# A macaron block with relative-position attention on one core: earlier value loads, last stores on two queues, means kept unnegated

## The chip, the cores and the metric

The kernel runs on one core of a Trainium2 chip. A core has a matrix engine (PE, with its weight loads listed as PEld), a vector engine (DVE), an activation engine (ACT), a general engine (POOL) and SP, which in this kernel only issues DMA transfers. Each engine works through its own list of instructions in order; semaphores make one engine wait for another or for a transfer. The metric is the time of one execution in microseconds of the device; the figure for a kernel is the median over runs. The profile is one execution, recorded by the hardware profiler.

## The reference

The input x has the shape (8, 1024, 256): 8 sequences of 1024 rows, 256 columns, in 32-bit floats. One block is computed, of three parts with a residual each:

```
x = x + 0.5 * ffn(layernorm(x))
x = x + attn(layernorm(x))
x = x + 0.5 * ffn(layernorm(x))

layernorm(x): (x - mean) / sqrt(var + 1e-5), over the 256 columns
ffn(y):  tanh(y @ W1 @ W2 @ W3 + bias)
attn(y): y = layernorm(y) * g + b;  q, k, v = y @ Wq + bq, y @ Wk + bk, y @ Wv + bv   (16 heads of 16)
         p = sinusoidal_positions @ Wp
         score = ((q + u_bias) . k  +  shift((q + v_bias) . p)) / 4
         softmax(score) @ v, heads put together, @ Wo + bo
```

`shift` is the reshaping trick in which a column of zeros is put before the position scores, the array is read with rows one longer, and the first row is dropped. The scores of one head are 8 x 1024 x 1024 numbers.

## The kernel before

**First stage (to about 300 us).** Eight groups of 128 rows of all 8 sequences are loaded (`load_x`, L250). A `Stats` object (L257) holds the layer norm's statistics of a group: DVE computes mean and variance (`bn_stats`, `bn_aggr`), and in `ends` (L269) a DVE instruction (L272) writes the negated means into a tile `n`; POOL computes 1/sqrt(var + eps) in two instructions (`rsqrt`, L104 to L106). `apply` (L284) lets POOL write (x + n) * r, one instruction for each of the 8 sequences, with n and r as per-partition scalars. This is done twice for each group ("a" ahead of the first feed-forward part, "b" ahead of the attention), 16 times in all. POOL also clears the tiles of the attention stage here (`UnitSet.clear`, L138, memsets at L140 and L143), and adds a constant row vector to x (L384). Queries, keys and values go to DRAM (qv_d, k_d, v_d), the residual goes to x1c_d.

**Attention stage.** A unit is one head with one quarter (row group `rg`) of the query rows: 64 units of 16 steps, so 1024 steps T. `step` (L1023) computes the scores of step T+2 in PSUM on PE, takes their row maxima on DVE (L934, L940, L947), and lets ACT exponentiate (L963) the scores of step T into the tile eT. `step` also issues one item of the list `loads` in each row maximum (`row_max`, L943): SP's transfers of the next unit's data, each made to follow that step's DVE reduction (L950). `fetch` (L1012) fills the list at the first step of each unit: six keys' transfers in five items, two items of position data, two of the values (`v`, 256 KB each, into the tile vt) and four of queries. In the last unit there is no next unit, so `k`, `p` and `q` are empty; the slices of them still are appended, as three empty items, and the values come as the fourth and fifth item. At the first step of the following unit, `emit_av` (L983) multiplies eT by vt on PE (L971), ACT copies the sums (L978) and SP stores them in h_d (L992). The values' tile has one buffer, so a unit's values are loaded after the unit before has been multiplied. While later units run, `post_ops` (L754) finishes the blocks (one of 8 sequences of one row group each, 32 in all) of the row group before: normalise by the softmax sums, output projection, residual, layer norm (`stats_dve`, L108, with the negated means at L117, and `apply`, L812), second feed-forward part, store.

**Last unit and last blocks (from L1072).** After step 1009 (the second of the last unit) SP gets, in program order, the load of the softmax sums of 15 heads (rc, L1075), the numerators of heads 0 to 7 (tn, L1087); then step 1010 runs; DVE inverts rc (L1094), SP stores it in r_d (L1095), loads the other numerators (tn), both sets of inverted sums (td, L1100, which wait for r_d) and the residual rows of the 8 last blocks (xr, L1106, in `load_rows` L728, 16 transfers of 128 KB). Then come steps 1011 to 1023. After them the last unit's av is formed in two halves of 4 sequences (L1136), and each half's 16 sums and 16 inverses are moved to the other heads' tiles by 4 + 4 small SP transfers (L1141, L1144). POOL multiplies numerators by inverses (L1117, and L1172 for the last heads), ACT and DVE split them into two 16-bit parts (L1123, L1129, L1173), PE projects them (`proj`, L1155). The 8 last blocks then pass through the remaining operations of `post_ops` as a pipeline (L1182 to L1191): DVE adds and takes statistics, POOL normalises, PE transposes and multiplies, ACT takes the tanh, then `fin` (L842) adds the result to xr, on ACT and POOL for blocks 0 to 4 and on DVE for 5 to 7, and `store` (L852) writes out by two SP transfers (`store_rows`, L734), one for each half of its rows, 128 KB each.

The order on each engine is the order in which the Python code calls the instructions; a framework adds the semaphores. DMA transfers use eight semaphores in turn, so that a transfer waits until the one eight places earlier has landed.

Of the kernel before, what the change touches and what calls it, by code (L numbers as in the profile page):

```python
# [10 lines left out]
F32 = mybir.dt.float32  # L11
AF = mybir.ActivationFunctionType
ALU = mybir.AluOpType
# [3 lines left out]
P = 128  # L17
NB = 8
# [14 lines left out]
NU = NTILE // UT  # L33
# [10 lines left out]
def macaron_kernel(  # L44
# [23 lines left out]
    nc = tc.nc  # L68
# [35 lines left out]
    def rsqrt(r, var):  # L104
        nc.gpsimd.tensor_scalar(r, var, 1.0, EPS, ALU.mult, ALU.add)
        nc.gpsimd.tensor_tensor(r, r, mhalf[:, : r.shape[1]], ALU.pow)  # L106

    def stats_dve(pool, xt, n, nm):  # L108
        st = pool.tile([P, n, 6], F32, tag="st" + nm, name="st" + nm)
        mv = pool.tile([P, n, 2], F32, tag="mv" + nm, name="mv" + nm)  # L110
        for b in range(n):
            nc.vector.bn_stats(st[:, b, :], xt[:, b, :])
        for b in range(n):
            nc.vector.bn_aggr(mv[:, b, :], st[:, b, :])
        r = pool.tile([P, n], F32, tag="r" + nm, name="r" + nm)
        nm_ = pool.tile([P, n], F32, tag="n" + nm, name="n" + nm)
        nc.vector.tensor_scalar_mul(nm_, mv[:, :, 0], -1.0)  # L117
        return nm_, r, mv

# [6 lines left out]
    class UnitSet:  # L128
        def __init__(self, pool, n):
            def t(name, shape):  # L130
                return pool.tile(shape, F16, tag=f"{name}{n}", name=f"{name}{n}")

            self.qc = t("qc", [KC, UT, 4, 32])
            self.q = t("q", [KR, UT + 1, NI * NB, 2])
            self.k = t("k", [KC, NI, 4, P])
            self.pg = t("pg", [KR, GW])
# [93 lines left out]
    if True:  # L230
        p2 = early.enter_context(tc.tile_pool(name="p2", bufs=2, side="right"))
# [25 lines left out]
        class Stats:  # L257
            def __init__(self, nm, xt):
                self.nm, self.xt = nm, xt
                self.st = p2.tile([P, NB, 6], F32, tag="st" + nm, name="st" + nm)  # L260
                self.mv = p2.tile([P, NB, 2], F32, tag="mv" + nm, name="mv" + nm)
                self.r = p2.tile([P, NB], F32, tag="r" + nm, name="r" + nm)
                self.n = p2.tile([P, NB], F32, tag="n" + nm, name="n" + nm)

            def rows(self, lo, hi):
                for b in range(lo, hi):
# [2 lines left out]
            def ends(self):  # L269
                for b in range(NB):  # L270
                    nc.vector.bn_aggr(self.mv[:, b, :], self.st[:, b, :])
                nc.vector.tensor_scalar_mul(self.n, self.mv[:, :, 0], -1.0)  # L272
                rsqrt(self.r, self.mv[:, :, 1])

            def again(self):
# [8 lines left out]
            def apply(self, tag):  # L284
                xn = p2.tile([P, NB, D], F32, tag=tag, name=tag, bufs=1)
                for b in range(NB):
                    nc.gpsimd.tensor_scalar(
                        xn[:, b, :], self.xt[:, b, :], self.n[:, b : b + 1],
                        self.r[:, b : b + 1], ALU.add, ALU.mult,
                    )  # L290
                return xn

# [368 lines left out]
        for I in range(NI - 2, -2, -1):  # L661
# [39 lines left out]
            for n in range(4):  # L701
                q = query(xTb, cvst[(I + 1) % 2], n % 2, n // 2)
                k = key(xTb, ks, n % 2, n // 2)
# [27 lines left out]
                t[:, e, :], src.rearrange("(k r) c -> k r c", r=P)[:, r : r + 16]  # L731
            )

    def store_rows(dst, t, rg):  # L734
        for e, r in ((0, 16 * rg), (1, 64 + 16 * rg)):
            nc.sync.dma_start(
                dst.rearrange("(k r) c -> k r c", r=P)[:, r : r + 16], t[:, e, :]
            )

# [14 lines left out]
    def post_ops(rg, b, sb, nb, pm, pt_, t):  # L754
        def new(name, shape, tag=None, dt=F32):
            t[name] = sb.tile(shape, dt, tag=tag or name, name=name, bufs=nb)
            return t[name]

        def load():
            num = new("num", [P, 2, 2 * P])  # L760
            den = new("den", [P, 2, 2 * P])
            for hh in range(2):
                hs = slice(8 * hh, 8 * hh + 8)
                nc.sync.dma_start(num[:, hh, :], h_d[rg, hs, 0:DH, b])
                nc.sync.dma_start(
                    den[:, hh, :],
                    r_d[rg, hs, b : b + 1, :].broadcast_to([8, DH, 2 * P]),
                )
            xr = new("xr", [P, 2, D])
            load_rows(xr, x1c_d[b], rg)  # L770

        def norm():
            nc.gpsimd.tensor_tensor(t["num"], t["num"], t["den"], ALU.mult)

        def hi1():
            new("hl", [P, 2, 2, 2 * P], dt=F16)
            nc.scalar.copy(t["hl"][:, 0], t["num"])

        def lo1():
            nc.vector.tensor_tensor(t["hl"][:, 1], t["num"], t["hl"][:, 0], ALU.subtract)  # L780

        def prod(ps, hl, w, tk, extra):
            n = 0
            for k in range(2):
                for a, c in ((0, 0), (1, 0), (0, 1)):
                    mm(  # L786
                        ps[:, tk, :], hl[:, a, k, tk * P : (tk + 1) * P], w[:, c, k, :],
                        start=n == 0, stop=n == 5 and not extra,
                    )
                    n += 1  # L790

        def proj():
            t["ps"] = pm.tile([P, 2, D], F32, tag=pt_, name="wops")
            for tk in range(2):
                prod(t["ps"], t["hl"], wo16, tk, False)

        def res():
            nc.vector.scalar_tensor_tensor(
                out=t["xr"], in0=t["ps"], scalar=1.0 / WS, in1=t["xr"], op0=ALU.mult,
                op1=ALU.add,  # L800
            )

        def projres():
            proj()
            res()

        def ln():
            if nb > 1:
                res()
            t["nm"], t["r"], t["mv"] = stats_dve(sb, t["xr"], 2, f"p{b % nb}")  # L810

        def apply():  # L812
            rsqrt(t["r"], t["mv"][:, :, 1])
            xn = new("pn", [P, 2, D])
            for k in range(2):
                nc.gpsimd.tensor_scalar(
                    xn[:, k, :], t["xr"][:, k, :], t["nm"][:, k : k + 1],
                    t["r"][:, k : k + 1], ALU.add, ALU.mult,
                )

        def trans():
            t["ps"] = pm.tile([P, 2, 2 * P], F32, tag=pt_, name="ptp")
            for c in range(2):
                for tk in range(2):
                    nc.tensor.transpose(  # L825
                        t["ps"][:, c, tk * P : (tk + 1) * P],
                        t["pn"][:, tk, c * P : (c + 1) * P], ident,
                    )
            new("pT", [P, 2, 2, 2 * P], "hl", F16)
            nc.scalar.copy(t["pT"][:, 0], t["ps"])  # L830
            nc.vector.tensor_tensor(t["pT"][:, 1], t["ps"], t["pT"][:, 0], ALU.subtract)

        def ffn():
            t["ps"] = pm.tile([P, 2, D], F32, tag=pt_, name="pff")
            for tk in range(2):
                prod(t["ps"], t["pT"], w16, tk, True)
                mm(t["ps"][:, tk, :], ones16, brow, start=False, stop=True)
            nc.scalar.activation(
                new("pth", [P, 2, D], "pn"), t["ps"], AF.Tanh, scale=1.0 / WS
            )  # L840

        def fin():  # L842
            if nb > 1 and b < NB - 3:
                nc.scalar.mul(t["pth"], t["pth"], 0.5)
                nc.gpsimd.tensor_tensor(t["xr"], t["xr"], t["pth"], ALU.add)
                return
            nc.vector.scalar_tensor_tensor(
                out=t["xr"], in0=t["pth"], scalar=0.5, in1=t["xr"],
                op0=ALU.mult, op1=ALU.add,
            )  # L850

        def store():  # L852
            store_rows(out[b], t["xr"], rg)

        return [
            (load, 4), (norm, 2), (hi1, 0), (lo1, 1), (projres, 0), (ln, 0), (apply, 4),
            (trans, 1), (ffn, 0), (fin, 1), (store, 1),
        ]

# [147 lines left out]
    preps, loads, stores = [], [], []  # L1007
# [4 lines left out]
    def fetch(u):  # L1012

        v = load_v(u) if u else []
        k, p = (f(u + 1) for f in (sets[(u + 1) % 2].load_k, sets[(u + 1) % 2].load_p)) \
            if u + 1 < NU else ([], [])
        q = sets[u % 2].load_q(u + 2) if u + 2 < NU else []
        loads.extend([pair] for pair in k[0:4])
        loads.append(k[4:6])
        loads.extend((p[0:2], p[2:4], v[0:1], v[1:2]))  # L1020
        loads.extend([pair] for pair in q)
# [51 lines left out]
    rg = units[-1][0]  # L1073
# [4 lines left out]
    def ttile(name, shape, dt=F32, tag=None):  # L1078
        return t1.tile(shape, dt, tag=tag or name, name=name)
# [3 lines left out]
    xr = ttile("xr8", [P, NB, 2, D])  # L1083
# [150 lines left out]
```

## Time and profile before

| | us |
|---|---|
| median of 3 runs | 2954.7 (2951.74 to 2957.57) |
| the profiled execution | 2962.17 |
| its span, first to last instruction | 2960.5 |
| PE busy | 2835.1 (96%) |
| DVE busy | 2188.1 (74%) |
| ACT busy | 1666.0 (56%) |
| POOL busy | 991.9 (34%) |
| mean granted PE clock | 0.984 of full |

Times in the views are from the start of the span. An engine's row names its line in the kernel, the operation, the tile written and the tiles read; "SPq" is SP's list of transfers, and its durations are those of issuing, not of moving the data. The number in brackets is how long the engine was idle before, and what ended that. The table of waits sums such idle times: who waited, for whom, how long, how often. The chain of waits follows the last instruction back to what released each step. A window gives each engine's busy time within a stretch, then the granted clock, the share of time in which the 16 DMA engines were busy, and the GB/s moved.

### The profile page before, as it was taken

The numbers are of one execution on the slowest core, as the hardware profiler recorded it, in microseconds if no ns is written. First come the engines' busy times: TensorE is split into PE (matmuls) and PEld (weight loads), VectorE is DVE, ScalarE is ACT, GpSimd is POOL, SyncE is SP. The second block draws the span as 40 slices with busy tenths as digits, with TensorE's granted clock in tenths as the row PEclk, the third lists the DMA queues.
The fourth block names the chain that finished last, engine by engine and source line by source line (L and its number), as shares of the span: only waits on it lengthen the run. The fifth ranks groups of instructions, "written<-read, shape, count | busy, mean of one in ns | idle before, by whom it ended". The sixth has DMA issues, their size and how long they took to land.

```text
span 2960.5 us, 157394 instructions
## 1 busy us (share of the span) xinstructions
PE 2835.1 (96%) x71212; PEld 2345.5 (79%) x71212; DVE 2188.1 (74%) x5001; ACT 1666.0 (56%) x3551; POOL 991.9 (34%) x1498
## 2 busy tenths in 40 slices
PE   7987999999999999999999999999999999999985
PEld 4755888888888888888888888888888888888874
DVE  7885777777777877877777787777777777777774
ACT  3655555555555655555555565556655556555552
POOL 8874222222222332332222332332222233232204
PEclk8999999999999999999999999999999999999997
DMA  4555322222223333322223323322223232222232
GB/s 146 185 164 177 87 69 68 65 66 67 67 68 76 85 85 86 85 76 68 66 66 78 84 81 86 83 70 70 70 70 78 82 87 81 83 68 65 67 88 70
DMA packets 333397, 250.63 MB, mean 85 GB/s; under 512 B 118885, under 2 KB 317142, under 8 KB 332246
## 3 DMA queue, kind: packets, MB, share of 16 engines
q1 hardware_dynamic: 332726, 240.56, 28.9%
q8 instruction: 558, 9.14, 1.3%
q14 instruction: 113, 0.93, 0.1%
HBM read 177.44 MB, written 62.78 MB: 81 GB/s over the span
## 4 chain that ended last, share of the span: by engine, by line
PE 83%; DVE 6%; DMA 2%; ACT 1%; issue 1%; SPq 1%; POOL 0%; ACTq 0%; DVEq 0%; POOLq 0%
PE s L1029 22%; PE s L1043 17%; PE av L971 15%; PE s L959 15%; PE s L1037 6%; DVE m L934 3%; PE mps L945 2%; PE pff L786 1%; DVE m L940 1%; PE wops L786 1%; DMA xr<-x1c_d 1%; ACT dg L952 1%; PE vv L467 1%; PE qq L454 1%; PE ptp L825 1%
## 5 line engine op out<-in xcount | busy, mean ns | idle before, releaser
L963 ACT ACTIVATE eT<-s 128x512 f32<-128x512 f32 x2048 | 1111.7, 594 | 992.3 <-PE s L959 990.7
L934 DVE TENSOR_REDUCE m<-s 128x128 f16<-128x512 f32 x2048 | 1406.3, 687 | 163.2 <-PE s L1029 30.6
L225 POOL TENSOR_SCALAR qc<-raw 48x256 f16<-48x256 f16 x507 | 328.6, 658 | 1229.0 <-PE s L1043 1191.4
L959 PE MATMUL s<-dg,many 128*128 128x512 f16 x2048 | 607.9, 378 | 33.0 <-ACT dg L952 33.0
L947 DVE TENSOR_REDUCE nm<-mps 128x1 f32<-128x128 f32 x1024 | 296.0, 289 | 450.3 <-PE mps L945 446.7
L1029 PE MATMUL s<-qc,k 114*128 114x32 f16 x16384 | 564.9, 176 | 18.9 <-DMA k<-c_d 18.9
L1037 PEld LDWEIGHTS <-k 114*128 114x128 f16 x8192 | 354.6, 96 | 244.3 <-issue 0.8
L1029 PEld LDWEIGHTS <-k 114*128 114x128 f16 x16384 | 487.9, 96 | 20.5 <-issue 19.1
L1029 PE MATMUL s<-q,pg 112*128 112x64 f16 (+3 forms) x12288 | 482.1, 184 | 0.5 <-issue 0.5
L1043 PE MATMUL s<-q,pg 112*128 112x64 f16 (+3 forms) x12288 | 481.7, 184 | 0.0
L971 PE MATMUL av<-eT,vt 128*32 128x256 f32 x8192 | 460.6, 382 | 19.8 <-DMA vt<-v_d 19.3
L952 ACT ACTIVATE dg<-ident,nm 128x128 f16<-128x128 f16 x1024 | 411.9, 402 | 77.0 <-DVE nm L947 66.4
L971 PEld LDWEIGHTS av<-eT,vt 128*32 128x32 f32 x8192 | 319.9, 139 | 133.6 <-issue 22.4
L1029 PEld LDWEIGHTS <-pg 112*128 112x128 f16 x12288 | 407.2, 97 | 0.6 <-issue 0.6
L1043 PEld LDWEIGHTS <-pg 112*128 112x128 f16 x12288 | 406.9, 97 | 0.0
L1037 PE MATMUL s<-qc,k 114*128 114x32 f16 x8192 | 364.5, 177 | 0.0
L1043 PE MATMUL s<-qc,k 114*128 114x32 f16 x8192 | 363.8, 177 | 0.0
L225 POOL TENSOR_SCALAR q<-raw 48x256 f16<-48x256 f16 x507 | 342.9, 687 | 20.1
L1043 PEld LDWEIGHTS <-k 114*128 114x128 f16 x8192 | 312.2, 96 | 0.0
L940 DVE TENSOR_TENSOR m<-m,m 128x128 f16<-128x128 f16 x1024 | 272.7, 266 | 35.2
L945 PE MATMUL mps<-ident,m 128*128 128x128 f16 x1024 | 222.5, 217 | 6.9 <-DVE m L940 4.5
L959 PEld LDWEIGHTS <-many 128*128 128x128 f16 x2048 | 127.3, 96 | 61.6 <-issue 61.2
(173 smaller groups left out, 1771.8 us busy)
## 6 DMA issues: line engine op xcount, KB each, us to landing
k<-k_d SPq DMA_DIRECT2D x128, 256.0 KB
vt<-v_d SPq DMA_DIRECT2D x128, 256.0 KB
raw<-qv_d SPq DMA_DIRECT2D x128, 144.0 KB
pg<-g_d SPq DMA_DIRECT2D x128, 132.5 KB
k<-k_d SPq DMA_DIRECT2D x128, 128.0 KB
h_d<-avs SPq DMA_DIRECT2D x126, 128.0 KB
qv_d<-cv SPq DMA_DIRECT2D x32, 288.0 KB
raw<-qv_d SPq DMA_DIRECT2D x128, 72.0 KB
```

What stands on the lines that cost most here:

```text
L225: nc.gpsimd.tensor_scalar(dst, src, 1.0, 0.0, ALU.mult, ALU.add)
L934: nc.vector.tensor_reduce(n, s_t[T][c].rearrange("p (j c) -> p c j", c=P), AX.X, ALU.max)
L940: nc.vector.tensor_tensor(n, n, m_t[T], ALU.max)
L945: mm(ps, m_t.pop(T), ident16, start=True, stop=True)
L947: r = nc.vector.tensor_reduce(nm, ps, AX.X, ALU.max, negate=True)
L952: nc.scalar.activation(dg, ident16, AF.Copy, scale=nm)
L959: mm(ps, many16, bass.AP(dg.tensor, dg.offset, [list(dg.ap[0]), [0, 4], [1, P]]), start=False, stop=True, skip_group_check=True,)
L963: nc.scalar.activation(eT[:, 4 * c : 4 * c + 4, :, t, :], ps.rearrange("p (j b n) -> p j b n", j=4, b=NB), AF.Exp,)
L971: mm(av[32 * c : 32 * c + 32, q, :], vt[:, j, :, 4 * q + c], eT[:, j, 4 * q + c].rearrange("p t n -> p (t n)"), start=j == 0, stop=j == NI ...
L1029: f()
L1037: f()
L1043: f()
```

## The change

Three edits. `fetch` puts the last unit's two value loads first into the list, without empty items, so that they are issued in the row maxima of steps 1009 and 1010 instead of 1012 and 1013; in the program's order the first now stands between the two h_d stores of the unit before, and the second between the first tn load and the r_d store, where both used to follow the sixteen xr loads. The second of the two output stores of each of the last three blocks is issued by ACT instead of SP; these are the only transfers that ACT issues. The layer norm's means are no longer negated by a DVE instruction into a tile of their own: POOL reads them from the statistics tile, and subtracts where it added. That takes out 48 DVE instructions, 16 of the first stage and 32 of the blocks.

```diff
@@ stats_dve
         r = pool.tile([P, n], F32, tag="r" + nm, name="r" + nm)
-        nm_ = pool.tile([P, n], F32, tag="n" + nm, name="n" + nm)
-        nc.vector.tensor_scalar_mul(nm_, mv[:, :, 0], -1.0)
-        return nm_, r, mv
+        return mv[:, :, 0], r, mv
@@ Stats
-                self.n = p2.tile([P, NB], F32, tag="n" + nm, name="n" + nm)
+                self.n = self.mv[:, :, 0]
...
-                nc.vector.tensor_scalar_mul(self.n, self.mv[:, :, 0], -1.0)
                 rsqrt(self.r, self.mv[:, :, 1])
...
                         xn[:, b, :], self.xt[:, b, :], self.n[:, b : b + 1],
-                        self.r[:, b : b + 1], ALU.add, ALU.mult,
+                        self.r[:, b : b + 1], ALU.subtract, ALU.mult,
@@ store_rows
-    def store_rows(dst, t, rg):
+    def store_rows(dst, t, rg, engines=None):
         for e, r in ((0, 16 * rg), (1, 64 + 16 * rg)):
-            nc.sync.dma_start(
+            (engines or (nc.sync,) * 2)[e].dma_start(
                 dst.rearrange("(k r) c -> k r c", r=P)[:, r : r + 16], t[:, e, :]
             )
@@ post_ops, apply and store
-                    t["r"][:, k : k + 1], ALU.add, ALU.mult,
+                    t["r"][:, k : k + 1], ALU.subtract, ALU.mult,
...
-            store_rows(out[b], t["xr"], rg)
+            last = nb > 1 and b >= NB - 3
+            store_rows(out[b], t["xr"], rg, (nc.sync, nc.scalar) if last else None)
@@ fetch
         q = sets[u % 2].load_q(u + 2) if u + 2 < NU else []
+        if u + 1 == NU:
+            loads.extend([pair] for pair in v)
+            return
         loads.extend([pair] for pair in k[0:4])
```

## The prediction

> **What bounds the kernel now.** I read the page first, then the table of waits, then SP's own timeline over the last 110 us, because the change touches loads, stores and one small instruction and nothing of TensorE's stream.
>
> The page, span and engines:
>
> ```profile
> span 2960.5 us, 157394 instructions
> PE 2835.1 (96%) x71212; PEld 2345.5 (79%) x71212; DVE 2188.1 (74%) x5001; ACT 1666.0 (56%) x3551; POOL 991.9 (34%) x1498
> ```
>
> PE is busy 96% of the span, and 40.00 of 40 us in every stretch of the stream I asked for. The change removes no PE work, so only what lies outside the stream can pay: the first 300 us, and the end, from 2850 us on. The table of waits has two long ones there:
>
> ```profile
> POOL tn L1117 <- DMA td<-r_d: 81.4, 1, 81.4
> ...
> PE av L971 <- DMA vt<-v_d: 19.3, 1, 19.3
> ```
>
> POOL's 81.4 us is idleness of an engine with nothing else to do. PE's 19.3 us is real: the last unit's attention-times-values products stand until their values land. SP's timeline says why (start, us, engine, line):
>
> ```profile
> 2849.58 2.50 SPq L992 DMA_DIRECT2D h_d<-avs  x2
> 2854.86 0.93 SPq L1075 DMA_DIRECT2D rc<-h_d  x1
> 2855.84 0.67 SPq L1087 DMA_DIRECT2D tn<-h_d  x1
> ...
> 2869.14 26.92 SPq L730 DMA_DIRECT2D xr<-x1c_d  x16
> 2896.24 1.08 SPq L950 DMA_DIRECT2D vt<-v_d  x2
> 2909.74 3.37 SPq L1141 DMA_DIRECT2D tn<-avs  x4
> 2913.21 2.43 SPq L1144 DMA_DIRECT2D td<-inv  x4
> 2915.74 2.43 SPq L1141 DMA_DIRECT2D tn<-avs  x4
> 2918.27 2.43 SPq L1144 DMA_DIRECT2D td<-inv  x4
> 2943.51 12.91 SPq L736 DMA_DIRECT2D out_dram<-xr  x16
> ```
>
> The two value loads sit behind sixteen loads of xr, which hold SP for 26.92 us. The chain of waits continues: 6.53 us until vt lands, av 6.41 us, its copy, then sixteen small transfers one after another until 2920.7, and from there the last blocks' work. Windows (PE, PEld, DVE, ACT, POOL busy; clock, DMA share, GB/s):
>
> ```profile
> 2850.00:2856.00 6.00, 5.43 (x176) 4.88 (x174) 3.38 (x8) 3.96 (x9) 0.00 (x0) 1.00 0.16 46
> 2857.00:2889.00 32.00, 21.40 (x567) 17.35 (x566) 26.17 (x52) 18.77 (x40) 0.00 (x0) 0.82 0.51 137
> ...
> 2948.00:2959.00 11.00, 3.11 (x29) 2.54 (x26) 3.75 (x4) 2.31 (x4) 3.11 (x3) 0.87 0.51 166
> ```
>
> The queue is nearly empty at 2850-2856 and runs steadily at 137 GB/s from 2857 to 2889.
>
> **Part 1, the value loads.** In the built order the first half stands between the two h_d stores, paced by the row maximum that DVE starts at 2850.41; the second between the first tn load (issued 2855.84) and the r_d store. What they are moved past: one h_d store, the rc load and both tn, td and all xr loads. Their pacing holds SP for nothing: that row maximum is done at 2850.70, before the h_d store behind the load has its data (2851.51); the next one starts at 2852.36, before the first tn load is issued.
>
> First cost: h_d's second half is 256 KB later in the queue. rc waits for it (3.31 us from issue to landing in the chain), and DVE waits for rc in order (3.98 us idle) with the row maxima behind it, so PE waits too (5.27 us). Ends: 0 (DMA share 0.16, there is room) and 1.6 us (256 KB at the 160 GB/s of 2826-2830, when the previous unit's values were loaded). I take 0.9, the middle, as the loads are issued within 0.8 us of each other.
> Second cost: the other 256 KB enters the full stretch. Ends 0 and 1.9 us (256 KB at 137 GB/s); I take 1.6, near the upper, since that stretch has no gap. Together the xr loads end 2.5 us later (0 to 3.5), at 2898.6 instead of 2896.06.
>
> Gain: what SP does next is the small transfers, and they need av. The last exponential ends at 2884.52; av is 3.54 us at full clock (half of the 7.08 in the chain for 128) or the 6.41 seen at half clock; copy 0.37: ready by 2892.2 with the 0.9. So SP, not av, sets the start: 2898.6 against 2909.74, **-11.1 us**. One small transfer took 1.42 us where the others took 0.53 to 0.63; not repeated, **-0.8**. Cover for the rest: av's second copy is behind ACT's casts (L1129), these behind POOL L1117 (4.63 us from td's landing at 2889.99, later by 2.5): copy done 2898.6, reciprocal (1.75) 2900.4; SP needs them at its 9th and 13th small transfer, 2903.7 and 2906.2. The 48 first projections took 5.25 us; at half clock 10.5, from 2898.5 at the latest to 2909.0, before the DVE chain needs PE again at about 2912. What is late next is therefore SP's xr issue itself. Part 1: **-11.9**, ends -14.5 (no delay) and -10.2 (3.5 delay; slow transfer again).
>
> **Part 2, the negations.** 48 DVE instructions go: 16 of L272, 32 of L117 (median 169 ns).
> In the stream 24 of these, 4.1 us of DVE beside a full PE: 0. In the last blocks POOL paces: 0.19 + 0.70 + 1.09 us and gaps, 2.25 per block, back to back from 2926.59; its start waits for the aggregate, not for the negation. 0; at most the 0.5 us of np in the chain.
> In the first 300 us, one of the sixteen was long. DVE and POOL timelines:
>
> ```profile
> 144.16 3.51 POOL L140 MEMSET k<- 114x4096 f16 x1
> 147.61 1.87 POOL L140 MEMSET pg<- 112x2120 f16 x1
> ...
> 145.94 3.56 DVE L272 TENSOR_SCALAR na<-mva 128x8 f32<-128x8 f32 x1
> 146.63 2.88 DVE L378 SCALAR_TENSOR_TENSOR xt<-th,xt 128x512 f32<-128x512 f32 x1
> ```
>
> L272 (else 0.17) and the two behind it end only with POOL's memsets, at 149.5; PE stood 1.32 + 0.59 us after it. But a DVE stall of that kind also follows from L378 beside POOL's L384 (5.31 us at 173.99, PE idle 3.15), and moving DVE earlier can make or unmake one. I take **-1.0**; ends -3.5 (the whole stall) and +4 (one more L378 stall).
> The Trainium skill, "SBUF — State Buffer", section "Who interferes with whom", says that a tensor_scalar in a two-port mode and any GpSimd instruction lock each other out, while a DVE instruction with two SBUF inputs is stopped only by a GpSimd instruction that reads SBUF. The rows fit (L378 took 0.67 beside the memset at 143.91), so by the page the 3.5 us go whole and the sum would be -17.3; by the rows, which show later stalls absorbing it, -14.8.
>
> POOL now subtracts instead of adding, in 128 + 64 instructions at 128x256 (553 ns median). No row has subtract in that form. As tensor-tensor, subtract took 1153 at 128x512, adding 1264: no dearer. The other pair at 128x256 (L570, multiply-multiply) is 482 ns. Ends -0.07 and +0.19 us each (741 is the two-input add of the same shape); I take 0, the nearest being the tensor-tensor pair.
>
> **Part 3, the last stores.** SP issued the last six from 2952.48 to 2956.42, 0.65 each, though the last result is ready at 2952.53:
>
> ```profile
> 2951.14 0.60 ACT L838 ACTIVATE pth<-pff 128x512 f32<-128x512 f32 x1 [0.87 <-PE pff L837]
> 2951.84 0.69 DVE L847 SCALAR_TENSOR_TENSOR xr<-pth,xr 128x512 f32<-128x512 f32 x1 [0.18 <-ACT pth L838]
> ```
>
> Three move to ACT: SP ends 3 x 0.65 = **-1.95** earlier, still after the result. On ACT the first of the three stands before the last tanh: it waits for block 5's result (2949.98) and issues, about 0.6 on SP, so 2950.9 against 2951.14: covered by 0.24 us; the other two come after it. In the built order each also waits until an early store (of blocks 0, 2 and 3, all issued by 2950.4) has landed. No row shows a store on ACT. Ends: -2.4 (three stores of 128 KB at 166 GB/s leave SP's queue) and +0.4 (the issue takes 1.20, the longest store row on SP, and delays the tanh).
> The Trainium skill, "DMA: Bandwidth & Descriptors", section "Issuing engines are not separate DMA queues", speaks against it: all issuers share 16 engines, and a second one saves only issue time. As the transfers go on for some 3 us after the last issue, by the page part 3 could be 0 and the sum -12.9. The DMA share of 0.51 there says there is room; I stay with the row.
>
> **Sum**: -11.9 - 1.0 - 1.95 = -14.85 us, against a profiled execution of 2962.17 us (span 2960.5 and 1.67 around it). That is 7.5 above the median of the three timed runs, 2954.7; the pieces are waits of fixed size, so I take them from the median: **2939.8**.
>
> **Rivals.**
> (a) Subtract is dearer on POOL: slower. POOL is busy 217 of the first 300 us, so half to all of the 128 instructions count, and all 16 in the last blocks. At the two-input price (+0.19) that is 80 to 144 x 0.19 = +15 to +27, giving 2955 to 2967. It cancels the gain from +0.19 each (+34%), and shows a slower kernel from about +0.26 if half counts. Against it: the tensor-tensor pair. Chance 0.06.
> (b) The wait changes place: both loads delay rc and xr in full, and the second reciprocal or a low clock on the projections takes 3 us more: 2939.8 + 1 + 3 = 2944. For it: every load is on one queue, and the clock was 0.50 at 2897-2903. Chance 0.17.
> (c) The stores are bound by transfer, or the tanh is held: part 3 is 0 to +0.4, 2942. Chance 0.14.
> (d) DVE and POOL collide once more early: +4 instead of -1, 2945. Chance 0.11.
> The forecast itself 0.52.
>
> **Range.** Low: all good ends, -14.5 - 3.5 - 2.4 = -20.4, 2934; with a shorter low-clock stretch in the last blocks (0.80 mean at 2925-2960) 2933. High: -10.2 + 4 + 0.4 = -5.8, 2949. Outside: (a), and sums beyond the ends. About 0.2% (6 us) is what a measurement here can tell from no change: the before runs alone spread over 5.8 us. Below 2948.8: the forecast, (b), (c), (d) but for their upper tails, 0.86. Within: those tails and part of (a), 0.08. Slower: the dear end of (a), and costs that no row shows, 0.06.
>
> **What the profile after would show.** Part 1: no wait of av for vt; vt's last two rows on SP near 2851 and 2857; the wait of DVE for rc 3.9 to 5.6 instead of 3.98; the first tn<-avs right behind the last xr, near 2899. Part 2: POOL's L287 and L816 rows at 553 ns; no 3.5 us DVE row near 146. Part 3: three store rows on ACT of about 0.6, PE's last matmul to the end 7.4 us instead of 9.4. Wrong would make it: POOL rows well above 553, xr ending past 2900, or a last tanh that starts later than PE's end.

## The result, and the profile after

The changed kernel takes 2992.18 us (median of 4 runs, 2990.86 to 2993.07); the kernel before took 2956.14 us beside it (4 runs, 2951.74 to 2957.63). The ratio is 1.0128 with a 95% interval of 1.0112 to 1.0144: some 38 us slower, where 15 us faster was forecast. (Here and below, microseconds given with a ratio are that ratio of the time before, not the difference of two medians.) The page of the changed kernel (span; busy time, share and instructions of each engine):

```profile
span 2991.3 us, 157315 instructions
PE 2844.4 (95%) x71212; PEld 2349.2 (79%) x71212; DVE 2164.9 (72%) x4953; ACT 1663.1 (56%) x3551; POOL 1122.5 (38%) x1498
```

DVE lost its 48 instructions. POOL has the same 1498 instructions as before but 130.6 us more work (991.9 before). The rows of the two normalisations on POOL (count: shortest/median/longest ns) name it; first the kernel before, then the changed one:

```profile
L287 POOL TENSOR_SCALAR xn<-xt,na,ra x64: 547/553/2032, 13.5 to 220.7; 128x256 f32<-128x256 f32 x64
L816 POOL TENSOR_SCALAR pn<-xr,np,rp x64: 553/555/576, 975.0 to 2945.2; 128x256 f32<-128x256 f32 x64
```

```profile
L284 POOL TENSOR_SCALAR xn<-xt,mva,ra x64: 1217/1222/2639, 12.9 to 273.0; 128x256 f32<-128x256 f32 x64
L813 POOL TENSOR_SCALAR pn<-xr,mvp,rp x64: 1222/1223/1231, 1021.8 to 2974.7; 128x256 f32<-128x256 f32 x64
```

The same shape takes 0.67 us more in each of the 192 instructions: 129 us, all but 2 us of POOL's extra work. The last xn starts at 273.0 instead of 220.7. What that does to the first stage shows in its windows (us; busy us of PE, PEld, DVE, ACT and POOL with counts; clock, DMA share, GB/s). Before:

```profile
50.00:100.00 50.00, 45.30 (x276) 29.13 (x277) 36.29 (x103) 24.36 (x43) 40.90 (x65) 0.88 0.41 131
150.00:200.00 50.00, 44.90 (x280) 26.76 (x279) 41.95 (x115) 25.40 (x44) 44.97 (x72) 0.93 0.49 158
```

Changed:

```profile
50.00:100.00 50.00, 34.47 (x203) 21.91 (x202) 28.57 (x72) 16.89 (x30) 47.88 (x57) 0.84 0.19 61
150.00:200.00 50.00, 36.98 (x221) 23.38 (x220) 26.03 (x78) 19.91 (x32) 48.58 (x49) 0.86 0.37 120
```

POOL is full from 50 us on (48 of 50), PE falls from 45 to 34 and 37. The timeline after shows PE waiting for one normalisation after another (start, us; in brackets the idle time before and its releaser):

```profile
60.29 6.05 POOL L284 TENSOR_SCALAR xm<-xt,mvb,rb 128x256 f32<-128x256 f32 x5
...
61.57 0.47 PE L349 MATMUL tp<-ident,xm 128*128 128x128 f32 x1 [6.82 <-POOL xm L284]
...
62.79 0.48 PE L349 MATMUL tp<-ident,xm 128*128 128x128 f32 x1 [0.74 <-POOL xm L284]
```

The first score matmul starts at 347.3 us instead of 299.9: 47.4 us lost. The two ends of the kernel can be set against this. From there to the last store of h_d the stream is 19 us shorter (2505.6 us from the first h_d store to the last before, 2486.4 after), which nobody forecast. From that last store (2851.5 before, 2879.8 after) to the end of the span it is 108.9 before and 111.5 after, and this nearly equal figure hides a gain and a loss. SP's own timeline after:

```profile
2877.89 0.58 SPq L990 DMA_DIRECT2D h_d<-avs  x1
2879.03 0.36 SPq L948 DMA_DIRECT2D vt<-v_d  x1
...
2885.38 0.39 SPq L948 DMA_DIRECT2D vt<-v_d  x1
...
2899.44 25.66 SPq L727 DMA_DIRECT2D xr<-x1c_d  x16
2928.98 3.49 SPq L1142 DMA_DIRECT2D tn<-avs  x4
```

The value loads now stand ahead of the xr loads, and av waits for no vt. The first small transfer (tn<-avs) comes 49.2 us after the last h_d store, 58.2 before: 9.1 us gained. Then, from the end of the small transfers to the end of the span, 51.3 us instead of 39.8: 11.5 us lost. The chain of waits of the changed kernel shows both halves:

```profile
2899.66 2.96 issue
...
2907.97 2.79 issue
...
2918.93 1.99 DVE m L938
...
2968.69 2.43 POOL pn L813 x2
2971.11 1.23 POOL xr L842
...
2972.71 0.72 POOL rp L106
2973.53 2.44 POOL pn L813 x2
...
2978.82 1.39 DVE xr L844
2980.23 1.23 ACTq L733
2981.51 0.61 ACT pth L835
```

The pairs of pn are 2.43 us where they were 1.09. At the very end a store issued by ACT (ACTq L733, 1.23 us) stands right before the last tanh. The two "issue" pieces, in which PE stood while the profile shows nothing that it waited for, lie in the last unit and come back below. So does m's 1.99 us (0.23 for most of these rows): it stands beside POOL's two tn multiplications (L1118), which take 4.64 us from 2918.49. In sum: +47.4 - 19.2 - 9.1 + 11.5 = +30.6, against 30.8 between the spans.

So the working theory was: the pair subtract-multiply costs 1222 ns on POOL where add-multiply costs 553, and POOL sets the pace in the first stage and in the last blocks. Rivals: reading the mean as every second column of the statistics tile is dear, not the subtraction; or the moved loads or the stores cost the time. And one question the change did not set out to ask: what made the stream 19 us shorter.

### The profile page after: what moved, and what is told of

Read it like the earlier page. It is cut to its first block, busy times and chain, and to the rows that moved or that the text cites. A ratio compares the mean times of both kernels' runs of the same rounds, so it can differ in the third digit from the quotient of the medians.

```text
span 2991.3 us, 157315 instructions
## 1 busy us (share of the span) xinstructions
PE 2844.4 (95%) x71212; PEld 2349.2 (79%) x71212; DVE 2164.9 (72%) x4953; ACT 1663.1 (56%) x3551; POOL 1122.5 (38%) x1498
## 4 chain that ended last, share of the span: by engine, by line
PE 82%; POOL 7%; DVE 6%; issue 1%; DMA 1%; ACT 1%; SPq 1%; ACTq 0%; POOLq 0%; DVEq 0%
PE s L1030 22%; PE s L1044 17%; PE av L969 15%; PE s L957 15%; PE s L1038 6%; DVE m L932 2%; PE mps L943 2%; POOL xm L284 2%; POOL xn L284 1%; PE pff L783 1%; PE wops L783 1%; ACT dg L950 1%; DVE stp L112 1%; POOL xt L381 1%; DVE xr L844 1%
## 5 line engine op out<-in xcount | busy, mean ns | idle before, releaser
L938 DVE TENSOR_TENSOR m<-m,m 128x128 f16<-128x128 f16 x1024 | 258.5, 252 | 35.1
```

What stands on the lines that cost most here:

```text
L938: nc.vector.tensor_tensor(n, n, m_t[T], ALU.max)
```

## The experiments

**The changed kernel, adding.** Only the operation changes; operands and waits stay.

```diff
-                        self.r[:, b : b + 1], ALU.subtract, ALU.mult,
+                        self.r[:, b : b + 1], ALU.add, ALU.mult,
...
-                    t["r"][:, k : k + 1], ALU.subtract, ALU.mult,
+                    t["r"][:, k : k + 1], ALU.add, ALU.mult,
```

> The changed kernel with one word put back at two places: the normalisations on POOL add the mean instead of subtracting it, still straight from the statistics tile. It computes (x + mean) * r where (x - mean) * r is wanted, so its output is not the reference's; every other instruction, operand and wait is that of the changed kernel. Theory (the pair subtract-multiply is what is dear on POOL): the POOL rows L284 and L813 fall from 1222 ns back to about 550, the first score matmul from 347 back to about 300 us, and the time to 2933 us if the units with blocks stay at 42.6 us, 2948 if they go back to 43.2. Rival (reading the mean as every second column of the statistics tile is what is dear): the rows stay at 1222 ns and the time at 2992. Rival (the value loads or the stores cost the time): the rows fall, but the time stays above 2980.

Measured: 2930.32 us, ratio to the kernel before 0.9905 (0.9886 to 0.9923), so 28 us faster. POOL's row of xn in this run (pn's: 558):

```profile
L284 POOL TENSOR_SCALAR xn<-xt,mva,ra x64: 547/556/2037, 13.4 to 221.1; 128x256 f32<-128x256 f32 x64
```

The operand is still every second column of the statistics tile, and the row is back at 556: the layout of the mean is not it, nor are the loads and the stores. First score matmul at 299.9. The units in which a block is finished take 42.7 us (43.4 before). So the one word is worth some 66 us (1.0128 less 0.9905 of 2956), and all the rest of the change together is a gain, larger than the forecast.

**What POOL charges for which pair.**

```diff
+    for b in range(8):
+        g.tensor_scalar(o[:, b, :], a[:, b, :], m[:, b : b + 1], r[:, b : b + 1], ALU.add, ALU.mult)
+    for b in range(8):
+        g.tensor_scalar(o[:, b, :], a[:, b, :], n[:, b : b + 1], r[:, b : b + 1], ALU.subtract, ALU.mult)
...
```

> A bench, not the layer: x is read, its row means and variances are taken, and then POOL runs the same 128x256 f32 operation (two scalars per row) eight times for each of eleven pairs of operations, four times each add-multiply and subtract-multiply at 128x128 and 128x512, then DVE runs both pairs, then POOL runs plain tensor-tensor add, subtract and multiply. None of attention and feed-forward is computed; the output holds x and the last result. Theory: add-multiply 550 ns, subtract-multiply 1220 ns, the same with the mean read as a contiguous column or as every second column; the difference grows with the width, so about 0.3 us more at 128x128 and 1.3 us more at 128x512; on DVE both pairs cost the same. Open beforehand, three ways: any pair with a subtract in it costs 1220 (then multiply-subtract is dear too), only a subtract in the first place does (then multiply-subtract is 550 and is a way out), or only multiply-add and add-multiply are quick and every other pair is dear (then multiply-multiply and add-add are 1220 as well). The tensor-tensor rows: 740 each, by the add of this shape in the last blocks of before (741).

Groups of the bench (busy us, mean ns of one). In this order: add-multiply with the mean from every second column (L96) and contiguous (L98); subtract-multiply likewise (L100, L102); multiply-add, multiply-subtract, multiply-multiply, add-add (L104 to L110); add-multiply and subtract-multiply at 512 (L122, L124); tensor-tensor add and subtract (L130, L132):

```profile
L96 POOL TENSOR_SCALAR o<-a,mv 128x256 f32<-128x256 f32 x8 | 4.3, 558 | 8.6 <-DVE mv L84 8.6
L98 POOL TENSOR_SCALAR o<-a,m,mv 128x256 f32<-128x256 f32 x8 | 4.3, 558 | 0.0
L100 POOL TENSOR_SCALAR o<-a,mv 128x256 f32<-128x256 f32 x8 | 9.7, 1224 | 0.0
L102 POOL TENSOR_SCALAR o<-a,m,mv 128x256 f32<-128x256 f32 x8 | 9.7, 1224 | 0.0
L104 POOL TENSOR_SCALAR o<-a,m,mv 128x256 f32<-128x256 f32 x8 | 4.3, 562 | 0.0
L106 POOL TENSOR_SCALAR o<-a,m,mv 128x256 f32<-128x256 f32 x8 | 9.7, 1228 | 0.0
L108 POOL TENSOR_SCALAR o<-a,m,mv 128x256 f32<-128x256 f32 x8 | 4.3, 563 | 0.0
L110 POOL TENSOR_SCALAR o<-a,m,mv 128x256 f32<-128x256 f32 x8 | 9.7, 1229 | 0.0
L122 POOL TENSOR_SCALAR w<-o,m,mv 128x512 f32<-128x512 f32 x4 | 3.1, 772 | 0.0
L124 POOL TENSOR_SCALAR w<-o,m,mv 128x512 f32<-128x512 f32 x4 | 8.3, 2075 | 0.0
L130 POOL TENSOR_TENSOR o<-a 128x256 f32<-128x256 f32 x8 | 5.8, 727 | 0.9 <-DVE o L128 0.9
L132 POOL TENSOR_TENSOR o<-a 128x256 f32<-128x256 f32 x8 | 5.7, 722 | 0.0
```

The third of the three guesses comes nearest, and is still one pair off: add-multiply, multiply-add and multiply-multiply are quick, and every other pair tried is dear, add-add too (the remaining three, subtract-subtract, add-subtract and subtract-add, have 1229 to 1232 ns). It isn't the subtraction as such. From 256 to 512 columns a quick pair grows by 0.8 ns a column ((772 - 558)/256), a dear one by 3.3 ((2075 - 1224)/256), so the penalty grows with the width; at 128 columns the two pairs took 0.57 and 0.80 us. Tensor-tensor forms don't tell: add and subtract cost the same there (727, 722). DVE shows no such penalty: in the bench, while POOL stood, its add-multiply took 0.40 us (L126) and its subtract-multiply 0.40 us (L128). The bench was executed once.

**The loads and the stores without the means, and each alone.** The kernel before with the value loads, or the stores, or both as in the change's diff:

```diff
+        if u + 1 == NU:
+            loads.extend([pair] for pair in v)
+            return
```

```diff
-            store_rows(out[b], t["xr"], rg)
+            last = nb > 1 and b >= NB - 3
+            store_rows(out[b], t["xr"], rg, (nc.sync, nc.scalar) if last else None)
```

> The kernel before with the value loads and the stores of the change, and the negated means kept. Theory: POOL rows 550 ns; the value loads bring about -9 us and the stores 0, so 2947 us (2944 to 2950); units with blocks stay at 43.4 us. By the steps of the prediction (-11.9 and -1.95): 2942.

> The kernel before with the value loads of the last unit alone moved. Theory: 2947 us, no wait of the last av matmuls for vt, and the same time as with the stores added to within 1 us. If the two new PE stalls of 2.96 and 2.79 us (instruction fetch) belong to the moved loads they show here too; if they belong to where the instructions of the whole program lie, they differ from the changed kernel's, and the time is nearer 2943.

> The kernel before with the stores of the last three blocks divided between SP and ACT alone. Theory (the ACT issues hold the last tanh and lengthen SP's issues): 2956 us, within 1 us of the kernel before, with ACT store rows of 0.6 to 1.2 us. By the prediction's step: 2954. If it is slower than 2957 the stores cost part of the loss.

These and the adding kernel share their runs of the kernel before (2960.6 us). Both parts: 2950.48, ratio 0.9969 (0.9954 to 0.9983). The loads alone: 2951.53, ratio 0.9969 (0.9956 to 0.9981), so 9 us faster (6 to 13). The stores alone: 2956.23, ratio 0.9993 (0.9979 to 1.0006): no difference that can be told, and none on top of the loads either.

In the profile of the loads alone it is 95.2 us from the last h_d store to the end, 108.9 before: 13.7 gained. (Over the kernels with the value loads unmoved and the quick operation in the last blocks, this stretch is 105.9 to 108.9, so the gain is 11 to 14.) With both parts it is 98.3; there two PE stalls of 2.35 and 3.54 us stand in the last unit, like the 2.96 and 2.79 of the changed kernel. The stalls are not the loads' doing, nor the stores': the stores alone have them (1.70 and 2.98 us) and the loads alone do not, but two kernels below with neither have them as well (1.19 and 2.17 us with the idle negation, 2.24 and 3.38 with the subtraction in half of the first stage).

The chain at the end with the stores alone says why they bring nothing:

```profile
2946.48 1.39 DVE xr L847
2947.89 1.23 ACTq L736
2949.16 0.61 ACT pth L838
```

ACT's first store waits for a result of DVE that took 1.39 us, then holds ACT for 1.23 us, and only then comes the last tanh. From the last result to the end of the span it takes 7.8 us, 8.0 before.

**The un-negated means in the stream alone.** The kernel before; only the 24 blocks finished inside the stream get the new form. The second kernel still makes DVE's negated mean in them, and nobody reads it. (In the code nb is 1 for the blocks inside the stream and larger for the last ones.)

```diff
-    def stats_dve(pool, xt, n, nm):
+    def stats_dve(pool, xt, n, nm, neg):
...
+        if not neg:
+            return mv[:, :, 0], r, mv
         nm_ = pool.tile([P, n], F32, tag="n" + nm, name="n" + nm)
...
-                    t["r"][:, k : k + 1], ALU.add, ALU.mult,
+                    t["r"][:, k : k + 1], ALU.add if nb > 1 else ALU.subtract, ALU.mult,
```

> The kernel before, with un-negated means and the subtracting normalisation only in the 24 blocks that are finished inside the stream of units; the first stage and the last eight blocks keep the negated mean and the add. Theory (taking the small negation out of DVE's order frees 0.8 us of each of these 24 units, and POOL's dearer operation is hidden there): units with blocks 42.6 instead of 43.4 us, first score matmul at 300, the rest as before: 19 us less than the kernel before. By the prediction's step (24 negations beside a full PE: 0) it takes the same time as before; if POOL's 1.3 us more per block delays the copies that the next unit needs, it is slower than before.

> The same, but DVE still makes the negated mean in those 24 blocks, and nobody reads it: DVE's work is that of before, POOL's that of the change. If the 0.8 us are DVE's, the units with blocks are back at 43.4 us and the time at that of the kernel before; if they come from POOL's longer operation moving its later copies away from DVE's two-input operations, the units stay at 42.6 and the time 19 us below.

Beside a kernel before of 2954.05 us: without the negation 2938.35, ratio 0.9943 (0.9925 to 0.9961), 17 us faster, units with blocks 42.6 us. With the idle negation 2948.68, ratio 0.9984 (0.9971 to 0.9998), 5 us faster, units with blocks 43.3 us. Most of the gain is therefore DVE's small instruction, 0.17 us long, and the dear operation on POOL is hidden here. The adding kernel says the same from the other side: quick operation, no negation, 42.7.

How 0.17 us become some 0.7 of the 0.8 (43.3 to 42.6 between these two kernels, 43.4 to 42.7 with the quick operation) shows when the matmuls of one such unit are laid side by side: the kernel before falls behind the changed one at exactly three of its 1102, by 0.22, 0.32 and 0.25 us, the first a score matmul s<-dg, the other two mps. DVE's timeline of that unit in the kernel before:

```profile
1016.88 0.30 DVE L114 BATCH_NORM_AGGREGATE mvp<-stp 128x2 f32<-128x6 f32 x2
1017.22 0.17 DVE L117 TENSOR_SCALAR np<-mvp 128x2 f32<-128x2 f32 x1
1017.29 0.69 DVE L934 TENSOR_REDUCE m<-s 128x128 f16<-128x512 f32 x1
1017.89 0.28 DVE L947 TENSOR_REDUCE nm<-mps 128x1 f32<-128x128 f32 x1
...
1020.79 0.71 DVE L940 TENSOR_TENSOR m<-m,m 128x128 f16<-128x128 f16 x1
```

and in the changed one:

```profile
1062.91 0.30 DVE L114 BATCH_NORM_AGGREGATE mvp<-stp 128x2 f32<-128x6 f32 x2
1063.13 0.66 DVE L932 TENSOR_REDUCE m<-s 128x128 f16<-128x512 f32 x1
1063.71 0.28 DVE L945 TENSOR_REDUCE nm<-mps 128x1 f32<-128x128 f32 x1
...
1064.62 0.41 DVE L938 TENSOR_TENSOR m<-m,m 128x128 f16<-128x128 f16 x1
```

Without L117 the next row maximum comes 0.2 us earlier, and PE, which stands 0.68 us for it (through ACT's dg), stands 0.46. Later in the same unit the kernel before has m L940 at 0.71 and 0.63 us where 0.23 is usual, each while POOL copies (L225); the 0.71 ends with the copy. PE's mps waits for them. In the changed kernel the same two fall at other moments and take 0.23 and 0.34 us. (It has stretched rows of its own, one of 0.41 just before these and one of 0.60 after them; the latter is 0.64 in the kernel before too, and PE falls behind at neither.) That the two stretched ones follow from DVE's 0.2 us of lateness rests on the kernel with the idle negation: with POOL's work as in the change it falls behind at the same three matmuls, by 0.22, 0.30 and 0.13 us, its two rows taking 0.69 and 0.52 us.

**The subtraction in the first stage, in half of it, and in the last blocks alone.** Each is the kernel before with the un-negated mean and the subtraction in one place; the half takes only the second normalisation (xm):

```diff
-                        self.r[:, b : b + 1], ALU.add, ALU.mult,
+                        self.r[:, b : b + 1], ALU.add if self.nm == "a" else ALU.subtract, ALU.mult,
```

> The kernel before with un-negated means and the subtracting normalisation in the first stage alone: 128 operations of 0.67 us more each, 86 us of POOL work. Theory (POOL has some 80 us to spare in the first 300 us, and the rest is on the path): first score matmul at 347 us, units with blocks 43.4, 47 us slower than the kernel before, ratio 1.016. Rival (the first stage is longer in the changed kernel for another reason as well, such as the value loads of another order): less than 40 us.

> The same for the second normalisation of each block of tokens only (xm), the first (xn) keeps its negated mean: 64 dear operations, 43 us of POOL work. If POOL's spare time is one reserve of about 39 us (86 less 47) that is used up first, this costs about 4 us; if the operation is in the chain of every block, half, so 23 us. First score matmul at 304 or at 323.

> The kernel before with the subtracting normalisation in the last eight blocks alone. Theory (POOL paces these blocks, 16 operations of 0.67 us): 10.7 us slower, ratio 1.0036, from the end of the small transfers to the end of the span 50.5 instead of 39.8 us. If the last blocks are paced by another engine, nothing.

Beside a kernel before of 2957.56 us: the whole first stage 3015.14, ratio 1.0205 (1.0186 to 1.0225), 61 us slower (55 to 67); half of it 2979.35, ratio 1.0082 (1.0059 to 1.0105), 24 us (17 to 31); the last blocks 2965.7, ratio 1.0037 (1.0022 to 1.0052), 11 us (7 to 15). First score matmul at 345.4 and 318.0 us.

The last blocks are as expected: 16 x 0.67 = 10.7, and 51.1 us from the end of the small transfers to the end of the span, 39.8 before. Their chain is POOL's own, rp and pn in turn:

```profile
2939.25 0.73 POOL rp L106
...
2940.07 2.42 POOL pn L818 x2
...
2942.85 0.73 POOL rp L106
```

The half speaks for a chain: 43 us of POOL work more cost 24, so there is no reserve that is used up first; by these runs 57% of the extra time is on the path, and 70% when all are dear. The whole first stage cost more than the 47 us read from the two profiles. Part of that is scatter of the kernel before: its first score matmul came at 300 us in the profile shown, but at 291 to 293 in five of the eight profiles whose first stage is that of the kernel before. One DVE row tells the two courses apart. First the kernel before, then the loads alone:

```profile
173.99 5.31 DVE L378 SCALAR_TENSOR_TENSOR xt<-th,xt 128x512 f32<-128x512 f32 x1
```

```profile
174.24 0.85 DVE L378 SCALAR_TENSOR_TENSOR xt<-th,xt 128x512 f32<-128x512 f32 x1
```

Both run beside POOL's L384. In the three profiles at 300 us this row takes 5.3 us, PE stands 3.2 us behind it, and the clock granted from 175 to 200 us is 0.86; in the five at 291 to 293 us it takes 0.7 to 1.2 us, and that clock is 1.00. What makes the row long in some executions is open, and so is whether it accounts for all of the 8 us. Under the dear operations the first score matmul came at 345 and 347 us, with long rows of this kind at other places.

**A version that keeps what pays.** The value loads, and the un-negated means in the stream's 24 blocks only:

```diff
+        if u + 1 == NU:
+            loads.extend([pair] for pair in v)
+            return
...
-                    t["r"][:, k : k + 1], ALU.add, ALU.mult,
+                    t["r"][:, k : k + 1], ALU.add if nb > 1 else ALU.subtract, ALU.mult,
```

> The kernel before with the value loads of the change and the un-negated means in the stream's 24 blocks only; no divided stores. If the parts add up (9 us for the loads, 19 for the units with blocks): 28 us less than the kernel before, ratio 0.990 to 0.991, beside 0.9905 for the changed kernel that adds.

Measured: 2931.92 us, ratio 0.9922 (0.9904 to 0.9939), 23 us faster than the kernel before (18 to 28). Units with blocks 42.6 us, 94.7 us from the last h_d store to the end. It beats both kernels; the 28 expected is at the edge of its interval.

The parts by their own runs: loads -9, stores -2 (not told from 0), stream -17, first stage +61, last blocks +11, together +44 with an uncertainty of some 10; the change as a whole is +38.

## Why the prediction was wrong, by its own steps

**The step that failed: "I take 0, the nearest being the tensor-tensor pair."** It is the price of POOL's subtraction. Taken: 0, ends -0.07 and +0.19 us each; measured: +0.67 (1222 against 553), in all 192 instructions. The conclusion from the tensor-tensor rows was right for that form, add and subtract do cost the same there (727 and 722 ns in the bench), though the two rows compared differed in the type they write (f16 and f32). But that form says nothing of this one: here the price hangs on the pair of operations. At 128x256 the kernel before has only quick pairs, add-multiply at 553 and multiply-multiply at 482 (that one with a single per-row scalar). At eight columns it did hold a hint, which the prediction passed over: an add-add (L628) took 0.33 us where a multiply-add (L105) takes 0.20.

```profile
40.15 0.33 POOL L628 TENSOR_SCALAR uvw<-uvw,uv 128x8 f32<-128x8 f32 x1
...
48.12 0.20 POOL L105 TENSOR_SCALAR qb<-qb 128x8 f32<-128x8 f32 x1
```

It says that pairs can differ in this form, not by how much at 256 columns. The upper bound was the second part of the error. Two inputs at the same shape (741) looked like the most that could be asked, and nothing in the trace limited it to that; an operation no row shows in its form needed a wider end, at least a doubling.

**Rival (a) was the right mechanism at a third of its price.** Half to all of the first stage's 128, and all 16 of the last blocks, at 0.67: (64 to 128) x 0.67 + 10.7 = 54 to 96 us of loss, against a gain of 15. Measured: 61 + 11, in the lower half. The sign hung on the one price alone, as the rival's own figure said (it cancels at +0.19); for that it had far too small a chance.

**"24 of these, 4.1 us of DVE beside a full PE: 0"** failed too, on the good side: -17 us. The stretches that showed 40.00 of 40 us of PE, from 2700 to 2820 us, had no block being finished in them. In the 24 units with one PE does wait for DVE (from 1000 to 1040 us it is busy 38.80 of 40), and the negation stood in that chain. The 4.1 us were no bound either, since the late DVE then met POOL's copies.

**"I take -1.0" for the first 300 us:** with the quick operation and no negations the first score matmul comes at 299.9. That profile has the long L378 row (5.25 us), so it is to be set against the three at 299.9 to 300.7 and not against those at 291 to 293. The 3.56 us row is gone; PE is 2.3 us further on at 151 us for it, and loses 2.7 us at 169 us to another wait for DVE: 0 in all by these single profiles, within the ends of -3.5 and +4. From the rule of the Trainium skill ("SBUF — State Buffer", section "Who interferes with whom") the prediction read that the 3.5 us would go whole. The rule describes the stall; it doesn't say what the path does with it, and here a later wait took it up. The dear end of +4 for one more stall at L378 looks too small: the courses with and without that long row lie 8 us apart.

**Part 1, -11.9:** right in mechanism; -9 us by the runs (6 to 13), a little short of its ends of 10.2 to 14.5, and 11 to 14 in the profile of the loads alone. Its first cost showed: PE stands 5.67 us behind rc with the loads alone, 5.27 before, so 0.4 where 0.9 was taken. The delay of 2.5 us for the xr loads did not: their issue ends 43.1 to 45.3 us after the last h_d store with the value loads moved, 42.7 to 45.8 without. What was late next was SP's xr issue in two kernels (0.2 us before the first small transfer, in the adding kernel and in the version that keeps what pays); in the changed kernel it was av, behind the two PE stalls (3.9 us after xr's issue).

**Part 3, -1.95:** 0 by the runs, as rival (c) said. The upper end had the mechanism, an issue of 1.20 that delays the tanh; ACT's three issues took 1.23, 0.87 and 0.62, and SP's own grew to between 0.76 and 1.24 meanwhile in the changed kernel. The margin of 0.24 us, on which the cover rested, was too thin for one row at 1.23. The Trainium skill ("DMA: Bandwidth & Descriptors", section "Issuing engines are not separate DMA queues") was the better guide here: it says that a second issuer brings no second set of DMA engines, and the time from the last result to the end stayed at 8 us.

**In the last blocks** the negation's removal was rightly put at about nothing (40.1 us from the small transfers to the end in the adding kernel, 39.8 before); POOL does pace, and that is why its dear operation was paid there in full, 10.7 us.

## What to carry to other kernels

When an edit changes only the operation of an instruction, its price is unknown until a row shows that operation in that form on that engine; the same operation in another form (tensor-tensor for tensor-scalar) is no evidence, and its upper end should be a multiple. A rewrite like this can be kept where its engine has time to spare and dropped where the engine paces: here the negation is worth removing inside the stream, by 17 us, and worth keeping in the first stage and the last blocks. No run here tried a form that is both right and quick on POOL without the DVE instruction, such as a multiply-add. Before a small instruction on a side engine is costed at nothing, look at a window in which it runs, not at one nearby in which the main engine happens to be full.

## What was not expected of the hardware

On POOL a tensor-scalar operation at 128x256 f32 takes 558 to 563 ns for add-multiply, multiply-add and multiply-multiply, and 1224 to 1232 ns for the six other pairs of add, subtract and multiply tried, add-add among them; at 512 columns it is 772 against 2075.

A 0.17 us instruction on DVE cost some 0.7 us of PE time in each of 24 units (43.3 against 42.6 us): 0.2 by its own place, the rest while DVE rows beside POOL's copies took 0.69 and 0.52 us instead of 0.23 and 0.34.

One DVE row beside POOL's L384 takes 5.3 us in three profiles of the same first stage and 0.7 to 1.2 us in five, and the two groups differ by 8 us in the first stage.

PE has two stalls of 1.2 to 3.5 us each in the last unit in five of the twelve profiles of the whole kernel (2.96 and 2.79 in the changed kernel, 2.35 and 3.54 with both parts, 1.70 and 2.98 with the stores alone, 1.19 and 2.17 with the idle negation, 2.24 and 3.38 with half of the first stage subtracting), and none in the others. They begin within 1.5 us of a 16 KB packet of instructions, before which none had come for 6.7 to 14.8 us. A late packet is not enough: the seven profiles without a stall all have two packets 9 to 11 us apart in that unit. The cause is open.
